# Segment attention with batch norm: bounds of the segments by products with a search matrix, and the first list ahead of the other tables

## The chip, the cores and the metric

The kernel runs on one core of a Trainium2 chip. The time is the device time of one execution in microseconds (us); the profile's span, from the first to the last instruction, is some microseconds shorter. The core has five engines that run their own instruction streams and meet at semaphores: PE (TensorE, matrix products), DVE (VectorE), ACT (ScalarE), POOL (GpSimd, which here issues gathers and scatters by index) and SP (SyncE, which here issues plain transfers).

## The reference

16,384 tokens with 256 features each carry a segment number from 0 to 7 (`bids`), in no order. The reference lets every token attend to the tokens that its segment holds in a padded table, and normalises the result over all tokens:

```python
q, k, v = feat @ Wq, feat @ Wk, feat @ Wv          # 32, 32 and 256 wide
starts = jnp.searchsorted(bids, jnp.arange(8))     # a binary search in bids as they stand
pos = jnp.arange(N) - starts[bids]
def pad(x): return jnp.zeros((8, 3072, x.shape[-1])).at[bids, pos].set(x)
scores = jnp.einsum('bld,bmd->blm', pad(q), pad(k))          # unset keys masked by -1e9
rp = jnp.einsum('blm,bmd->bld', softmax(scores), pad(v))
t = rp[bids, pos] @ Wt
tn = (t - t.mean(0)) / jnp.sqrt(t.var(0) + 1e-5) * gamma + beta
return feat + jax.nn.relu(tn)
```

Because `bids` isn't sorted, the search ends where a binary search in an unsorted row happens to end, and most positions fall outside the table of 3,072 slots or wrap to its other end. A token that owns a slot is called an owner; each segment has some 500 to 700 of them here. All other tokens read a slot at one of a table's edges.

## The kernel before

**Tables.** `bids` lies in a tile of 128 partitions by 128 tokens (`b_i`, `b_f`). For each segment a start is found by two binary searches on DVE (`search`, L758 to L764): seven rounds over the first tokens of the partitions (`lo_p`), a product that fetches the row found (`ps_row`), and seven rounds within that row (`lo_j`); the result is `st_bc`. From it follow each token's position (`pos`), the owners (`own`, L794 to L803), how often each row of the result is read (`reads`, written to DRAM at L811), and for each segment a running count of its owners (`lcx`, nine scans at L816, the ninth for tokens that lost their slot to another). Two products give each partition's first rank and the totals (`ps_c`, L822). The largest total, read into registers as `n_max` (L857), decides at L863 whether this path or a general one runs.

**Lists.** `load_list(e)` makes the list of segment e. DVE marks which partition holds each rank (`oh`, L906 to L912), PE multiplies these marks with `lcx` in FP32 (`pc`, L936), DVE compares counts with ranks (`upto`, L947) and adds up the token's number (`idx`, L952). POOL then gathers the tokens' rows (`xs`) and their counts of reads (`reads_r`) from DRAM, one indirect DMA for 128 rows (L892).

**Attention.** Segments are worked one after the other, in tiles of 128 tokens: four tiles if there are fewer than 512 owners, else six. `tc.Switch` over four bits (twice, for segments 0 to 3 and 4 to 7) picks code for these lengths. `project(b)` transposes the rows (`px`, L974, copied to `xT` by ACT and DVE), forms queries and keys (`pqk`, L985) and values (`pv`, L1004); `scores` forms `s` and ACT its exponentials (`pr_a`, `pr_b`); `sums` forms a tile's weighted sum (`po`, L1051), divides it (`rdens`), subtracts a reference row (`tk`, L1056), and adds its first and second moments, weighted by `reads_r`, to `acc` (L1059 and L1065, with ACT's square between). `reference_row` makes that row as the mean of segment 0's values.

The program writes segment 0's list, project(0), its first scores, the reference row and the list of segment 1; then for each segment b: project(b+1), load_list(b+2), attend(b), first scores of b+1, and at b = 0, 1, 2 and 4 the tables of edges and of the losers. A scheduler orders each engine's instructions from that; between the arms of a Switch nothing moves.

**End.** The moments give a scale and a shift (`sums`, L1320); then all of `feat` passes through SBUF in 16 transfers of 1 MB each way, the edges' value is added by a product with a selection matrix (`hot`), and POOL scatters the owners' rows over the result.

Of the kernel before, what the change touches and what calls it, by code (L numbers as in the profile page):

```python
# [9 lines left out]
F32 = mybir.dt.float32  # L10
# [8 lines left out]
P = 128  # L19
NB = 8  # L20
# [511 lines left out]
def segment_attention_bn_kernel(  # L532
# [43 lines left out]
    with ExitStack() as short:  # L576
# [13 lines left out]
        nc.vector.memset(eps_t, EPS)  # L590
        nil = keep.tile([P, 1], F32, name="nil")
        nc.vector.memset(nil, 0.0)
        ones = keep.tile([P, P], F32, name="ones")
        nc.vector.memset(ones, 1.0)
# [3 lines left out]
        lcx = keep.tile([P, NL, J + 2], F32, name="lcx")  # L598
        cend = keep.tile([P, NL], F32, name="cend")
        n_bc = keep.tile([P, NL], F32, name="n_bc")  # L600
        iota_r = keep.tile([P, FW], F32, name="iota_r")
        rcol = keep.tile([P, FT], F32, name="rcol")
        irow = keep.tile([P, P], F32, name="irow")
        pcol = keep.tile([P, 1], F32, name="pcol")
        emod = keep.tile([P, 1], F32, name="emod")
        later_part = keep.tile([P, 2], F32, name="later_part")
        st_bc = keep.tile([P, NB], F32, name="st_bc")
        arm_i = keep.tile([1, 1], I32, name="arm_i")
        tiles_i = keep.tile([1, NB // PART], I32, name="tiles_i")
        ident = keep.tile([P, P], F32, name="ident")  # L610
        ecol = keep.tile([P, NB], F32, name="ecol")
        b_f = keep.tile([P, J], F32, name="b_f")

# [20 lines left out]
        def tmp(name):  # L634
            return keep.tile([P, J], F32, name=name)

        pos, below, above, own = tmp("pos"), tmp("below"), tmp("above"), tmp("own")
        cbeg = keep.tile([P, NL], F32, name="cbeg")

        def over_j(x, n=NB):  # L640
            return x.unsqueeze(2).to_broadcast([P, n, J])

        def over_e(x, n=NB):
            return x.unsqueeze(1).to_broadcast([P, n, J])
# [4 lines left out]
        with ExitStack() as prep:  # L649
            pp = prep.enter_context(tc.tile_pool(name="prep", bufs=1))  # L650
            pps = prep.enter_context(tc.tile_pool(name="prep_ps", bufs=1, space=PSUM))

            b_i = pp.tile([P, J], I32, name="b_i")
            bids2 = bids.rearrange("(p j) -> p j", j=J)
            nc.sync.dma_start(b_i, bids2)
            PS = LMAX // J
            bs_i = pp.tile([P, J], I32, name="bs_i")
            nc.vector.memset(bs_i, -1)
            nc.sync.dma_start(bs_i[0 : P - PS, :], bids2[PS:P, :])
            br_i = pp.tile([P, J], I32, name="br_i")  # L660
            nc.vector.memset(br_i, -1)
            nc.sync.dma_start(br_i[PS:P, :], bids2[0 : P - PS, :])
            wv_sb = pp.tile([P, DH, D], F32, name="wv_sb")
            nc.scalar.dma_start(wv_sb, wv.rearrange("(h p) m -> p h m", p=P))
            wt_sb = pp.tile([P, DH, D], F32, name="wt_sb")
            nc.scalar.dma_start(wt_sb, wt.rearrange("(h p) m -> p h m", p=P))
            for i, w in enumerate((wq, wq, wk, wk)):
                nc.scalar.dma_start(wqk[:, :, ts(i, DQ)], w.rearrange("(h p) m -> p h m", p=P))
            nc.scalar.dma_start(gamma_bc, gamma.unsqueeze(0).to_broadcast([P, D]))
            nc.scalar.dma_start(beta_bc, beta.unsqueeze(0).to_broadcast([P, D]))  # L670


            def iota_f(dst, pattern, base, mult, shape, name):
                raw = pp.tile(shape, I32, name=name)
                nc.gpsimd.iota(raw, pattern=pattern, base=base, channel_multiplier=mult)
                nc.vector.tensor_copy(dst, raw)
                return raw

            iota_f(irow, [[1, P]], 0, 0, [P, P], "irow_i")
            pcol_i = iota_f(pcol, [[0, 1]], 0, 1, [P, 1], "pcol_i")  # L680
            make_identity(nc, ident)
            m3 = pp.tile([P, NB, J], F32, name="m3")
            w3 = pp.tile([P, NB, J], F32, name="w3")
            o3 = pp.tile([P, NL, J], F32, name="o3")
            iota_f(ecol, [[1, NB]], 0, 0, [P, NB], "ecol_i")
            tok = pp.tile([P, J], F32, name="tok")
            iota_f(tok, [[1, J]], 0, J, [P, J], "tok_i")
            iota_f(rcol, [[P, FT]], 0, 1, [P, FT], "rcol_i")
            iota_f(iota_r, [[1, FW]], 0, 0, [P, FW], "iota_r_i")
            emod_i = pp.tile([P, 1], I32, name="emod_i")  # L690
            nc.vector.tensor_scalar(emod_i, pcol_i, NE - 1, None, ALU.bitwise_and)
            nc.vector.tensor_copy(emod, emod_i)
            part_i = pp.tile([P, 1], I32, name="part_i")
            nc.vector.tensor_scalar(part_i, pcol_i, 3 * NE, None, ALU.bitwise_and)
            nc.vector.tensor_scalar(later_part[:, 0:1], part_i, NE, None, ALU.is_ge)
            nc.vector.tensor_scalar(later_part[:, 1:2], part_i, 2 * NE, None, ALU.is_ge)

            def zero(x):
                nc.scalar.copy(x, nil.to_broadcast([P, x.shape[1]]))

            for b in range(NB):
                zero(xs[:, ts(b, FT), :].rearrange("p t d -> p (t d)"))
            for b in range(NB):
                zero(tk[:, b * FT + TMIN : (b + 1) * FT, :].rearrange("p t d -> p (t d)"))
            for x in (acc, E, xL, L):
                zero(x.rearrange("p t d -> p (t d)"))
            nc.vector.memset(reads_r, 0.0)
            nc.vector.memset(rdens, 1.0)
            nc.vector.memset(ridL, NB * FW)
            powers = pp.tile([1, NB], F32, name="powers")  # L710
            for b in range(NB):
                nc.gpsimd.memset(powers[:, b : b + 1], float(1 << (b % PART)))

            tri = pp.tile([P, P], F32, name="tri")
            nc.vector.tensor_scalar(tri, irow, pcol, None, ALU.is_gt)
            later = pp.tile([P, J], F32, name="later")
            nc.vector.tensor_scalar(later, irow, 0.0, None, ALU.is_gt)


            wvT = pp.tile([P, DH, D], F32, name="wvT")  # L720
            for m in range(DH):
                ps = pps.tile([P, D], F32, tag="w", name=f"ps_wvT{m}")
                for h in range(DH):
                    nc.tensor.transpose(ps[:, ts(h, P)], wv_sb[:, h, ts(m, P)], ident)
                nc.scalar.copy(wvT[:, m, :], ps)
            for h in range(DH):
                ps = pps.tile([P, D], F32, tag="w", name=f"ps_wvt{h}")
                for m in range(DH):
                    nc.tensor.matmul(
                        ps, wvT[:, m, ts(h, P)], wt_sb[:, m, :], start=(m == 0), stop=(m == DH - 1)  # L730
                    )
                nc.scalar.copy(wvt[:, h, :], ps)

            nc.vector.tensor_copy(b_f, b_i)
            bs_f = pp.tile([P, J], F32, name="bs_f")
            nc.vector.tensor_copy(bs_f, bs_i)

            first = pp.tile([P, NB], F32, name="first")  # L740
            nc.vector.tensor_copy(first, b_f[:, 0:1].to_broadcast([P, NB]))
            ps_first = pps.tile([NB, P], F32, tag="s", name="ps_first")
            nc.tensor.matmul(ps_first, first, ident, start=True, stop=True)

            less = pp.tile([NB, P], F32, name="less")
            hit = pp.tile([NB, P], F32, name="hit")
            mid = pp.tile([NB, 1], F32, name="mid")
            go = pp.tile([NB, 1], F32, name="go")
            lo_p = pp.tile([NB, 1], F32, name="lo_p")
            lo_j = pp.tile([NB, 1], F32, name="lo_j")  # L750

            def at_mid(where):
                nc.vector.scalar_tensor_tensor(
                    hit, irow[0:NB, :], where, less, ALU.is_equal, ALU.mult, accum_out=go
                )

            def search(lo):
                nc.vector.memset(lo, 0.0)  # L758
                w = P // 2
                while w:  # L760
                    nc.vector.tensor_scalar(mid, lo, float(w), None, ALU.add)
                    at_mid(mid)
                    nc.vector.scalar_tensor_tensor(lo, go, float(w), lo, ALU.mult, ALU.add)
                    w //= 2  # L764

            nc.vector.tensor_scalar(less, ps_first, pcol[0:NB, :], None, ALU.is_lt)
            search(lo_p)
            sel = pp.tile([NB, P], F32, name="sel")
# [713 lines left out]
```

## Time and profile before

| what | value |
|---|---|
| time | 438.07 us, median of 3 (436.2 to 439.6) |
| span of the profiled run | 432.9 us |
| busy: PE, DVE, POOL, ACT | 313.1, 274.3, 167.8, 110.1 us |
| mean granted clock of PE | 0.799 |
| first gather of rows | at 40.20 us |
| first queries and keys | at 51.30 us |
| first transfer of the last stage | at 311.02 us |

Busy time is the time in which an engine had an instruction under way. A slice's digit is its busy share in tenths. In a timeline the first number is the start and the second the duration in us, `xN` the number of merged instructions (an FP32 product is recorded as two), and brackets give the idle time of the engine just before and what ended it. PEclk is the clock that PE was granted, 1.00 being full.

### The profile page before, as it was taken

The page shows a single profiled execution, that of the slowest core. Times are in us where ns is not written, and L with a number is a line of the kernel's source. Part 1 is how long each engine was busy: PE and PEld are TensorE (multiplying, and loading weights), DVE is VectorE, ACT ScalarE, POOL GpSimd, SP SyncE. Part 2 cuts the span into 40 slices and gives each one's busy share as a digit, 9 for nine tenths or more (in the row PEclk, how much of TensorE's full clock was granted, in tenths as well). Part 3 has the DMA queues.
Part 4 walks back from the last instruction along what each step waited for, and adds up shares of the span by engine and source line. Part 5 has one row for each costly group of instructions (what it writes and reads, how often), then busy time and mean ns, then how long its engine had stood idle before and what let it go on. Part 6 is the DMA issues. An engine that isn't in the chain of part 4 may idle for free. (4 is left out here: it accounts for less than half of the span.)

```text
span 432.9 us, 4300 instructions
## 1 busy us (share of the span) xinstructions
PE 313.1 (72%) x1195; PEld 197.4 (46%) x1195; DVE 274.3 (63%) x801; ACT 110.1 (25%) x205; POOL 167.8 (39%) x179
## 2 busy tenths in 40 slices
PE   1143684996697999999599989999706888989200
PEld 0022253763363687587267757776302333334000
DVE  6796124996962267556457954646479866596950
ACT  5930131230222333342343135144010111111000
POOL 2002714868037046527001844701020053776770
PEclk9996597998697799999579999999855675555555
DMA  4000101030013013003202301102495999999940
GB/s 101 1 6 14 30 1 47 12 115 17 4 29 113 0 38 104 21 24 106 61 0 85 114 26 36 59 24 86 128 420 241 341 380 402 401 388 415 381 162 2
DMA packets 21485, 53.38 MB, mean 123 GB/s; under 512 B 6606, under 2 KB 14112, under 8 KB 17322
## 3 DMA queue, kind: packets, MB, share of 16 engines
q1 hardware_dynamic: 10474, 24.98, 16.1%
q10 hardware_dynamic: 4224, 17.70, 10.3%
q0 software_dynamic: 6720, 10.02, 7.5%
q14 instruction: 51, 0.42, 0.3%
q8 instruction: 16, 0.26, 0.3%
HBM read 26.67 MB, written 29.92 MB: 131 GB/s over the span
## 5 line engine op out<-in xcount | busy, mean ns | idle before, releaser
L892 POOL DMA_INDIRECT xs<-in_r_feat,idx x48 | 53.3, 1110 | 115.4 <-DVE upto L947 98.0
L1051 PE MATMUL po<-vs,pr_a 128*128 128x257 f32 x320 | 78.3, 391 | 2.9 <-ACT pr_a L1023 2.3
L1413 POOL DMA_INDIRECT out<-tk,idx x48 | 47.3, 985 | 54.4 <-DMA out<-f 36.7
L1051 PEld LDWEIGHTS po<-vs,pr_a 128*128 128x128 f32 x320 | 59.3, 193 | 17.3 <-issue 4.4
L892 POOL DMA_INDIRECT reads_r<-reads_of,idx x48 | 51.8, 1078 | 14.6 <-issue 14.6
L1385 PE MATMUL pf<-y,hot 48*128 48x256 bf16 x128 | 35.2, 381 | 23.0 <-DVE f L1396 11.4
L1396 DVE TENSOR_TENSOR f<-f,pf 128x512 f32<-128x512 f32 x48 | 30.9, 683 | 16.7 <-PE pf L1385 16.6
L1018 PE MATMUL s<-q,k 32*128 32x512 f32 (+1 forms) x128 | 36.8, 593 | 6.0 <-DVE q L995 6.0
L1004 PE MATMUL pv<-wvt,xT 128*128 128x256 f32 x168 | 40.8, 398 | 0.0
L974 PE MATMUL px<-ident,xs 128*128 128x128 f32 x84 | 20.4, 350 | 26.5 <-DMA xs<-in_r_feat,idx 18.7
L1004 PEld LDWEIGHTS pv<-wvt,xT 128*128 128x128 f32 x168 | 32.9, 199 | 9.9 <-ACT q L996 2.8
L1385 PEld LDWEIGHTS <-hot 48*128 48x128 bf16 x128 | 13.7, 118 | 51.0 <-issue 47.6
L1390 PE MATMUL pf<-f,ident 128*128 128x256 f32 x64 | 35.4, 663 | 1.4 <-DMA f<-in_r_feat 1.4
L1064 ACT ACTIVATE sq<-tk 128x256 f32<-128x256 f32 x40 | 16.7, 417 | 69.8 <-DVE tk L1056 62.7
L974 PEld LDWEIGHTS px<-ident,xs 128*128 128x128 f32 x84 | 11.7, 170 | 42.6 <-issue 19.6
L1023 ACT ACTIVATE pr_a<-s,mask 128x512 f32<-128x512 f32 x40 | 24.7, 687 | 17.8 <-PE s L1018 17.7
L1394 ACT COPY f<-pf 128x512 f32<-128x512 f32 x16 | 9.4, 586 | 72.1 <-PE pf L1390 46.8
L978 DVE COPY xT<-px 128x256 f32<-128x256 f32 x21 | 8.9, 422 | 29.5 <-PE px L974 29.5
L985 PE MATMUL pqk<-xT,wqk 128*128 128x512 f32 (+1 forms) x52 | 25.4, 634 | 0.1
L1051 PE MATMUL po<-vs,pr_b 128*128 128x257 f32 x96 | 21.8, 381 | 0.3 <-DVE tk L1056 0.3
L992 DVE COPY k<-pqk 32x128 f32<-32x128 f32 x42 | 12.2, 291 | 14.0 <-PE pqk L985 13.1
L1390 PEld LDWEIGHTS pf<-f,ident 128*128 128x128 f32 x64 | 15.4, 292 | 12.2 <-issue 7.6
(240 smaller groups left out, 431.6 us busy)
## 6 DMA issues: line engine op xcount, KB each, us to landing
f<-in_r_feat SPq DMA_DIRECT2D x16, 1024.0 KB, 10.0
out<-f ACTq DMA_DIRECT2D x16, 1024.0 KB, 9.8
t_rows<-tk SPq DMA_DIRECT2D x4, 768.0 KB, 4.7
t_rows<-tk SPq DMA_DIRECT2D x4, 512.0 KB, 2.9
eb<-edge_of SPq DMA_DIRECT2D x16, 96.0 KB, 2.4
t_rows<-tk SPq DMA_DIRECT2D x4, 256.0 KB, 2.1
xs<-in_r_feat,idx POOLq DMA_INDIRECT x48, 2.8
reads_r<-reads_of,idx POOLq DMA_INDIRECT x48, 2.4
```

What stands on the lines that cost most here:

```text
L892: nc.gpsimd.indirect_dma_start(out=dst, out_offset=None, in_=table, in_offset=bass.IndirectOffsetOnAxis(ap=ind, axis=0), bounds_check=n - ...
L974: nc.tensor.transpose(px[:, ts(t, P)], xs[:, b * FT + t0 + t, ts(h, P)], ident)
L985: nc.tensor.matmul(pqk[:, 0:w], wqk[:, h, :], xT[:, h, own_c], start=(h == 0), stop=(h == DH - 1),)
L1004: nc.tensor.matmul(pv[:, t, :], xT[:, h, ts(t0 + t, P)], wvt[:, h, :], start=(h == 0), stop=(h == DH - 1),)
L1018: nc.tensor.matmul(s[:, i, 0:w], k[g, t // 4, :], q[g, c : c + w], start=True, stop=True)
L1023: nc.scalar.activation((pr_b if c else pr_a)[:, t, 0:w], s[:, i, 0:w], AF.Exp, bias=mask[:, m : m + 1],)
L1051: nc.tensor.matmul(po, pr[:, t, ts(r, P)], v[:, t, :], start=(t == 0), stop=(t == T - 1))
L1064: nc.scalar.activation(sq, tk[:, at, :], AF.Square)
L1385: nc.tensor.matmul(pf[:, u, :], hot[r, g % (NG // 2), i + u, :], y3[r, :], start=True, stop=not on_pe,)
L1390: nc.tensor.matmul(pf[:, u, :], ident, two[:, u, :], start=False, stop=True)
L1396: nc.vector.tensor_add(two, two, pf)
L1413: w = nc.gpsimd.indirect_dma_start(out=out, out_offset=bass.IndirectOffsetOnAxis(ap=idx[:, at : at + 1], axis=0), in_=y, in_offset=None, b ...
```

## The change

Four things are changed, all for the time until the rows of the first segments are on chip.

1. The two binary searches become products. A binary search visits a known set of places, so a matrix `path` of 128 by 128 entries tells, for the comparisons of all places at once, which end the search reaches: the place where the product equals its least possible value (`path_min`).
2. Ownership of segment e is decided without `pos`: two comparisons of the token's place with bounds from the segment's start (`begin`, `end`), for one segment at a time, so that segment 0's count, list and gathers come ahead of all other tables. The order on DVE and PE is written out by hand for this part; `positions` (with `reads`) follows project(0), the losers' count `others` follows segment 0, and the branch on `n_max` goes: the same condition now ends in `bad`, which is looked at after the end as before. `reference_row` takes one tile instead of six. Segments 0 and 1 and 2 have their lists made ahead of the Switch, and segment b's stage makes the list of b+3.
3. The counts `lcx`, the marks `oh` and the segment masks `m3`, `o3` are BF16 instead of FP32 (ranks are split into a high and a low part), and `token_tables` reuses `m3` and `o3`.
4. The moments of segment b are added in the stage of segment b+1 (`moment`), save for segments 3 and 7, which end a Switch. The gathers of `reads_r` are a part of their own (`load_reads`). Zeroing the two unused tiles of `tk` moves from the start into the stage of each short segment.

```diff
-            def search(lo):
-                nc.vector.memset(lo, 0.0)
-                w = P // 2
-                while w:
-                    nc.vector.tensor_scalar(mid, lo, float(w), None, ALU.add)
-                    at_mid(mid)
-                    nc.vector.scalar_tensor_tensor(lo, go, float(w), lo, ALU.mult, ALU.add)
-                    w //= 2
+        def visits(name, less):
+            ps = ps_o.tile([P, NB], F32, tag="po", name=f"ps_{name}")
+            nc.tensor.matmul(ps, path, less, start=True, stop=True)
+            return ps
+
+        def ends(name, ps):
+            sel = tmp(name, NB, BF16)
+            nc.vector.tensor_scalar(sel, ps, path_min, None, ALU.is_equal)
+            return sel
...
+        def owners(e):
+            one = slice(e, e + 1)
+            nc.vector.scalar_tensor_tensor(
+                o3[:, e, :], place, begin[:, one], m3[:, e, :], ALU.is_ge, ALU.mult
+            )
+            nc.vector.scalar_tensor_tensor(
+                o3[:, e, :], irow_b, end[:, one], o3[:, e, :], ALU.is_lt, ALU.mult
+            )
+            count(e, o3[:, e, :])
...
-        lcx = keep.tile([P, NL, J + 2], F32, name="lcx")
+        lcx = keep.tile([P, NL, J + 3], BF16, name="lcx")
...
-                    oh = fw.tile([P, FW], F32, tag="oh", name=f"oh_{e}", bufs=1)
+            oh = fw.tile([P, FW], BF16, tag="oh", name=f"oh_{e}")
...
+        with tc.manual_schedule(engines={mybir.EngineType.DVE, mybir.EngineType.PE}):
+            paths()
...
+            sel_p = ends("sel_p", ps_p)
+            ps_row = ps_o.tile([P, NB], F32, tag="po", name="ps_row")
+            nc.tensor.matmul(ps_row, b_b, sel_p, start=True, stop=True)
...
+            owners(0)
+            ps_0 = ranks(0, 1)
+            nc.vector.tensor_copy(st_bc, ps_st)
+            owners(1)
+            ranks_kept(0, 1, ps_0)
+            oh = list_masks(0, FT)
+            pcs = [list_places(0, h, oh) for h in range(FT // 3)]
+            for e in range(2, 4):
+                owners(e)
+            for h, pc in enumerate(pcs):
+                list_tokens(0, h, pc)
+            weights()
+            for e in range(4, NB):
+                owners(e)
+            ps_1 = ranks(1, NB)
...
+            ranks_kept(1, NB, ps_1)
+            load_list(1)
+        tc.no_sync_barrier()
...
         project(0, FT)
         first_scores(0)
         reference_row()
+        positions()
+        load_reads(0)
+        load_list(2)
+        load_reads(1)
...
+                    if b + 3 < NB:
+                        load_list(b + 3)
                     if b + 2 < NB:
-                        load_list(b + 2, FT, xs[:, ts(b + 2, FT), :])
+                        load_reads(b + 2)
+                    if i:
+                        for u in range(T[i - 1]):
+                            moment((b - 1) * FT + u)
                     attend(b, T[i])
```

## The prediction

> **What bounds the kernel now.** I read the slices first, then the windows by stage, then the timelines of PE, POOL and DVE. The slices cut 432.9 us into 40 parts of 10.8 us:
>
> ```profile
> PE   1143684996697999999599989999706888989200
> POOL 2002714868037046527001844701020053776770
> DMA  4000101030013013003202301102495999999940
> ```
>
> Three regimes show. Slices 1 to 4: PE nearly idle, DVE at work. Slices 5 to 28: PE busy with a few holes. From 310 us: the DMA row at 9. The windows (length, then busy time of PE, PEld, DVE, ACT and POOL, granted clock, DMA share, GB/s) price them:
>
> ```profile
> 8.50:22.00 13.50, 1.45 (x5) 0.77 (x5) 10.36 (x66) 13.50 (x16) 0.00 (x0) 1.00 0.02 3
> 76.00:100.00 24.00, 22.51 (x97) 15.21 (x96) 23.81 (x66) 6.80 (x15) 17.30 (x15) 0.96 0.20 62
> 160.00:190.00 30.00, 29.99 (x141) 21.70 (x141) 15.59 (x51) 10.38 (x21) 15.07 (x16) 1.00 0.17 50
> 310.00:433.00 123.00, 70.58 (x196) 29.84 (x196) 83.54 (x144) 11.17 (x18) 53.23 (x54) 0.53 0.81 316
> ```
>
> The start is a serial chain on DVE; segment 0 fills DVE (23.8 of 24 us); later segments fill PE (30.0 of 30); the end, 123 us, is bound by DMA, begins after the last segment, and the change leaves it alone. So a microsecond counts if it moves the last segment's end. What PE waits for on its way there (start, duration, operation, idle before it):
>
> ```profile
> 51.30 4.15 PE L985 MATMUL pqk<-xT,wqk 128*128 128x512 f32 x8
> 67.34 1.50 PE L936 MATMUL pc<-lcx,oh 128*128 128x130 f32 x12
> 73.25 0.45 PE L974 MATMUL px<-ident,xs 128*128 128x128 f32 x1 [4.42 <-DMA xs<-in_r_feat,idx]
> 75.05 0.90 PE L974 MATMUL px<-ident,xs 128*128 128x128 f32 x3 [1.35 <-DMA xs<-in_r_feat,idx]
> 102.32 0.47 PE L974 MATMUL px<-ident,xs 128*128 128x128 f32 x1 [2.47 <-DMA xs<-in_r_feat,idx]
> 112.53 2.07 PE L1018 MATMUL s<-q,k 32*128 32x512 f32 x2 [4.84 <-DVE q L995]
> 135.97 0.90 PE L974 MATMUL px<-ident,xs 128*128 128x128 f32 x3 [2.69 <-DMA xs<-in_r_feat,idx]
> ```
>
> Real work begins at 51.30 (queries of segment 0); four later waits are for gathered rows, one is for DVE. POOL and DVE tell why:
>
> ```profile
> 40.20 1.20 POOL L892 DMA_INDIRECT xs<-in_r_feat,idx  x1 [5.29 <-DVE idx L952]
> 70.11 1.00 POOL L892 DMA_INDIRECT xs<-in_r_feat,idx  x1 [14.40 <-DVE upto L947]
> 75.15 0.62 DVE L906 TENSOR_SCALAR oh<-iota_r,lcx 128x768 f32<-128x768 f32 x1 [4.39 <-issue]
> ```
>
> The first row gather waits until 40.20 for `idx`; segment 1's until 70.11, since its list products stand behind all of project(0) on PE. The 4.39 us is the Switch on DVE; the new kernel keeps it.
>
> [...]the trace has FP32 only (twelve records of `pc` in 1.77 us at full clock, at 153.66). [...]the trace's 128x1024 products take 1,210 to 1,227. [...]the pair of `s` took 2.07 us after the 4.84 us hole and 1.13 elsewhere[...].[...]
>
> **Part 1, the start (to the first gather).** Before: two binary searches, 14 rounds of 0.74 us on DVE (8.6 to 20.7), then `pos` (1.23 + 1.93), ownership, nine scans and the n_max branch, all ahead of list 0. After, in the built order: ten path operations (1.3 to 3.1; small ones 0.18 apart, 128x128 ones 0.2 to 0.3), then four DVE-PE-DVE trips (`ps_min`, `sel_p`, `ps_row`, `sel_j`) and the pair `ps_st`. FP32 trips of this size take 0.37 (`selT`) to 0.69 us (`ps_row`); I take 0.4 to 0.5 in BF16. With 0.15 to 0.3 us operations between: `begin`/`end` at 7.5. owners(0): 0.3 + 0.3 + 0.42 = 1.0, to 8.6; owners(1) covers the `ranks` trip, to 9.7; five small copies, to 10.3; list masks 0.69 + 1.03, to 12.0; valid and mask, owners(2) and (3), 2.3, to 14.3; the first half list (as 38.43 to 39.91 before, one subtraction more) 1.9, to 16.2. **First gather 16.4 for 40.2: 23.8 us earlier.** The eight zero copies of `xs` (1.38 us apart on ACT) start near 2.5, so segment 0's slot is clear in time.
>
> **Part 2, to the queries of segment 0.** Six gathers 1.3 us apart end at 23.9 and land at 25.1, no longer interleaved with `reads`. But DVE's fixed order puts ahead of `xT`: the second half list (to 18.0), owners(4) to (7), 4.1 (22.1), ranks 1.2 (23.3), the masks of list 1, 1.7 (25.0), its tokens, 4.0 (29.0), then small bits and the 1.23 us product of `positions` (30.7). The three DVE `xT` copies are split by its 1.93 us reduction and by 0.9 of masks: they end at 31.1, 33.4 and 34.6. The weight products (two chains of 2.1 us, from about 17 when ACT ends its zeros) hide before `ps_1`. **Queries at 34.7 for 51.3: 16.6 us earlier**; 7 of the 23.8 are given back.
>
> **Part 3, to segment 1's transposes.** From the queries to the end of `pr0` took 16.2 us (67.5). Now `pr0` has one tile instead of six: 3.4 falls to about 0.6, so 13.4, to 48.1. Then list 2's BF16 products (0.7 for 1.5), its tokens on DVE and the Switch, the same 7.7 us as before (67.5 to 75.15): DVE enters segment 0 at 55.8, **19.3 us earlier**. List 1's rows (gathers 27.3 to 35) are there, so the 1.35 us wait goes too; DVE sets the pace.
>
> **Part 4, segments 0 and 1, bound by DVE.** From 75.15 to the queries of segment 2 at 113.5, DVE was busy about 34.8 us and idle 3.6. The built order of the arm these lengths take (4, 4, 6, 6 tiles: the two `pr_b` groups at 164 and 198) moves segment 0's eight moment operations behind those queries (3.3), drops the two 1024-wide `m3t`, `o3t` (2.3), adds others() and a second `lr` (1.7): about 31 us, and the `k` copies no longer alternate with table products. s(2) starts at about 86 for 112.5: **26.5 earlier**. POOL must follow: `reads` is written near 42 to 44, twelve `reads_r` gathers take 15.6 (to 60), list 2's six to 68; its transposes come near 74. Enough by 6 us.
>
> **Part 5, segments 2 to 7, bound by PE.** List 3 is now gathered a segment earlier, so the 2.69 us hole and the half clock behind it (pqk 5.37 for 2.7, s 2.07 for 1.13: 3.6) go: 6.3. Segment 1's list products save 1.1; its moments and edge tables now follow in one run beside PE (about +1). Lists 5, 6, 7 and the short one save 1.1 each where PE is full: 3.9. Moments a segment later cost DVE the same work; the last segment still has its own, so the tail is equal. Zeroing `tk` (0.53 us each) moves to ACT, which is a quarter busy, but two copies stand ahead of `xT` at the second Switch: +0.6. Sum: 26.5 + 1.1 - 1 + 6.3 + 3.9 - 0.6 = **36.2 us**.
>
> 438.1 - 36.2 = 401.9: **402 us**.
>
> **Rivals.** (a) *The head start stops at the DVE-bound part*: `reads` lands late, POOL serves twelve reads ahead of list 2, PE meets a new hole with half clock in segment 1, or table work again cuts up `k`. Then the 19.3 us of part 3 are kept and little else: 438.1 - 19.3 = 419. For it: DVE at 23.8 of 24 us; against: 6 us of slack. (b) *More*: BF16 quickens masks, owners and segment tests (half of some 6 us ahead of the queries), and PE, without holes, saves the half clock in segment 2 (pv 7.55 for 5.45, s 2.07 for 1.13: 3 us) and twice 2 us at the second Switch: 402 - 10 = 392. (c) *Slower*: PE, packed more densely, is granted less. At 0.83, as between 100 and 160 us, some 200 us of PE-bound work grow by 200 x (1/0.83 - 1) = 41: 402 + 41 = 443. Against it: full clock from 160 to 190 with no pause.
>
> **How the numbers follow.** Forecast 402: 0.65. (a) 419: 0.20. (b) 392: 0.12. (c) 443: 0.03. Unknowns: BF16 trips, 0.3 to 0.69 over five trips, is 2 us;[...] POOL's gathers, 1.0 each or stretched to the 2.85 seen at 98.30, a few us. With (a) and (b) inside: 390 to 419. Faster by over 1%: 0.95; within: 0.02; slower: 0.03.
>
> **What would show it.** Right: first gather near 16, first 512-wide `pqk` near 35, segment 0's DVE work from 56, no wait for `xs` after segment 0, transfers at 9 tenths from about 275 for the same 123 us. Wrong: PE waiting for `xs` of segment 2, a DVE wait on `reads_r` ahead of the moments, PEclk under 9 in segments 3 to 6, or a last stage longer than 123 us.

## The result, and the profile after

The changed kernel takes **389.85 us** (median of four runs, 386.95 to 398.45), the kernel before 437.13 beside it: a ratio of 0.889, 95% interval 0.881 to 0.897. Here and below, ratios and the times of the experiments leave out runs over 1.5% above the fastest of the same kernel; one of these four was such a run. The forecast was 402, between 390 and 419: the change gave more than forecast. The span fell from 432.9 to 386.6 us, by 46.3, where the forecast summed 36.2. The slices of the changed kernel (a slice is 9.7 us now):

```profile
PE   1347849889999999769997999974058877897100
POOL 3257477888747735600285000013000527776770
PEclk9986959999999999957999999995555785555555
DMA  5011002121502301310251010217949999999820
```

PE is at work from the fourth slice on, the DMA row reaches 9 some 40 us earlier, and the clock row shows what the forecast priced too low: from slice 7 to 17 it stays at 9. The 5 and 7 behind it are the second Switch, as before. The windows put numbers to it. First the kernel before (DVE's entry into segment 0 to the second Switch; segment 3's transposes and queries within it), then the changed kernel for the same work, and its end stage; the columns are those of the windows above.

```profile
75.15:203.50 128.35, 115.87 (x481) 81.85 (x481) 82.70 (x281) 36.02 (x76) 65.51 (x60) 0.91 0.16 48
...
130.01:146.37 16.36, 13.67 (x33) 6.64 (x33) 4.45 (x21) 2.47 (x6) 8.18 (x9) 0.69 0.23 74
```

```profile
54.00:160.00 106.00, 99.25 (x453) 71.07 (x453) 81.48 (x307) 35.42 (x75) 73.08 (x66) 0.97 0.21 62
...
97.39:105.60 8.21, 8.21 (x31) 4.30 (x31) 7.15 (x28) 2.23 (x6) 6.41 (x6) 1.00 0.51 151
...
263.30:386.60 123.30, 67.91 (x198) 29.24 (x198) 83.71 (x145) 11.17 (x18) 53.36 (x54) 0.56 0.80 315
```

Where PE slowed down, the granted clock was 0.50: in the kernel before from 112.53 to 117 and from 135.97 to 142, in the changed one from 50 to 58 and from 168.02 to 173. There a pair of scores took 2.07 us for 1.12. That is called half clock here; in the experiments it is mostly read from durations such as these. A mean of 0.91 over 128 us is then some 23 us at half clock (2 x 0.09 x 128.35); 0.97 over 106 us is some 6. For nearly the same products PE was busy 115.87 us and is busy 99.25: 4.9 of these 16.6 us are the list products, and 8 of the rest (half of 23 less 6, an estimate) are that clock. The timelines of PE, POOL and DVE, at the places shown before:

```profile
32.60 4.29 PE L915 MATMUL pqk<-xT,wqk 128*128 128x512 f32 x8
...
83.93 1.12 PE L948 MATMUL s<-q,k 32*128 32x512 f32 x2 [1.75 <-DVE q L925]
84.98 5.45 PE L934 MATMUL pv<-wvt,xT 128*128 128x256 f32 x24
...
97.39 0.66 PE L904 MATMUL px<-ident,xs 128*128 128x128 f32 x4 [0.42 <-DVE wE L1097]
...
102.75 2.85 PE L915 MATMUL pqk<-xT,wqk 128*128 128x512 f32 x8
```

```profile
16.66 1.25 POOL L821 DMA_INDIRECT xs<-in_r_feat,idx  x1 [12.55 <-ACT L L716]
```

```profile
54.00 0.79 DVE L834 TENSOR_SCALAR oh<-iota_r,cbeg 128x768 bf16<-128x768 f32 x1 [4.52 <-issue]
```

No wait for `xs` follows segment 0. The hole (idle time of PE) ahead of segment 2's scores is 1.75 us for 4.84, and the products behind it run at full clock (1.00 from 83.93 to 90.43). The account, by the starts of the same work in both traces:

| stretch | forecast gain | measured |
|---|---|---|
| to DVE's entry into segment 0 (75.15, 54.00) | 19.3 | 21.2 |
| on to the scores of segment 2 (112.53, 83.93) | 7.2 | 7.4 |
| on to segment 3's transposes (130.01, 97.39) | 0.1 | 4.0 |
| on to the end of segment 3's 512-wide queries (146.37, 105.60) | 6.3 | 8.2 |
| on to the second Switch (203.50, 159.96) | with the one but next: 3.9 | 2.8 |
| the second Switch, to the end of segment 5's 512-wide queries (222.50, 178.94) | -0.6 | 0.0 |
| on to the last `e_late`, a product of the last segment (306.61, 258.99) | see above | 4.1 |
| the rest (span 432.9, 386.6) | 0 | -1.3 |

So less than half of the gain lies ahead of segment 0's attention, where the change was aimed.

In the comparisons of the experiments below the kernel before took 455 to 470 us and the changed one 415 to 422, and the profiles of the changed and the edited kernels have idle stretches of 3 to 14 us whose release isn't recorded, above all behind the first Switch. What causes them was not found. The gain there is 37 to 40 us, where the first comparison had 49 (437.1 less 388.5). Each experiment is therefore read against the changed kernel of its own comparison where there is one, and by stretches without such idling.

### The profile page after: what moved, and what is told of

The parts are those of the page before. It is cut to its first block, busy times and chain, and to the rows that moved or that the text cites. A ratio compares the mean times of both kernels' runs of the same rounds, so it can differ in the third digit from the quotient of the medians.

```text
span 386.6 us, 4158 instructions
## 1 busy us (share of the span) xinstructions
PE 284.2 (74%) x1135; PEld 179.7 (46%) x1135; DVE 266.8 (69%) x792; ACT 107.9 (28%) x201; POOL 173.4 (45%) x180
## 5 line engine op out<-in xcount | busy, mean ns | idle before, releaser
L821 POOL DMA_INDIRECT xs<-in_r_feat,idx x48 | 58.6, 1220 | 66.3 <-DVE upto L871 36.6
L821 POOL DMA_INDIRECT reads_r<-reads_of,idx x48 | 50.9, 1060 | 21.5 <-issue 12.8
L1429 PE MATMUL pf<-y,hot 48*128 48x256 bf16 x128 | 33.8, 365 | 25.1 <-DVE f L1440 13.4
L934 PE MATMUL pv<-wvt,xT 128*128 128x256 f32 x168 | 38.7, 383 | 0.0
L934 PEld LDWEIGHTS pv<-wvt,xT 128*128 128x128 f32 x168 | 31.3, 190 | 8.6 <-ACT q L926 2.1
L1434 PE MATMUL pf<-f,ident 128*128 128x256 f32 x64 | 33.3, 628 | 2.2 <-DMA f<-in_r_feat 2.2
L948 PE MATMUL s<-q,k 32*128 32x512 f32 (+1 forms) x128 | 32.4, 570 | 2.9 <-DVE q L925 2.9
L978 ACT ACTIVATE sq<-tk 128x256 f32<-128x256 f32 x40 | 16.6, 417 | 62.8 <-DVE tk L994 56.2
L904 PE MATMUL px<-ident,xs 128*128 128x128 f32 x84 | 18.1, 333 | 17.3 <-DVE xT L908 8.0
L904 PEld LDWEIGHTS px<-ident,xs 128*128 128x128 f32 x84 | 10.9, 164 | 29.9 <-issue 12.8
L993 DVE RECIPROCAL rdens<-po 128x1 f32<-128x1 f32 x40 | 6.5, 164 | 23.6 <-PE po L989 23.5
L821 POOL DMA_INDIRECT E<-t_rows,eidx x1 | 1.1, 1108 | 43.5 <-issue 43.5
L1434 PEld LDWEIGHTS pf<-f,ident 128*128 128x128 f32 x64 | 14.6, 277 | 12.7 <-issue 6.9
```

Of the source, the lines that this page charges most:

```text
L821: nc.gpsimd.indirect_dma_start(out=dst, out_offset=None, in_=table, in_offset=bass.IndirectOffsetOnAxis(ap=ind, axis=0), bounds_check=n - ...
L904: nc.tensor.transpose(px[:, ts(t, P)], xs[:, b * FT + t0 + t, ts(h, P)], ident)
L934: nc.tensor.matmul(pv[:, t, :], xT[:, h, ts(t0 + t, P)], wvt[:, h, :], start=(h == 0), stop=(h == DH - 1),)
L948: nc.tensor.matmul(s[:, i, 0:w], k[g, t // 4, :], q[g, c : c + w], start=True, stop=True)
L978: nc.scalar.activation(sq, tk[:, at, :], AF.Square)
L1429: nc.tensor.matmul(pf[:, u, :], hot[r, g % (NG // 2), i + u, :], y3[r, :], start=True, stop=not on_pe,)
```

## The experiments

**The changed kernel again**, to see whom the idle stretches belong to.

> The changed kernel once more, as the measure for the runs beside it on the same chip. The four runs ahead of this one ran on a chip where the kernel before took 469.6 us, against 437 to 438 elsewhere, with idle stretches of 3 to 13 us behind the first Switch for which the profile names no cause of the program. My theory (those stretches belong to that chip's executions, the kernel before has them too): the ratio to the kernel before is 0.889 as in the first comparison, or a few per cent closer to one where the stretches are there. Rival (they belong to the edited kernels): the changed kernel is free of them on any chip.

Measured: 419.5 us, 456.6 before, ratio 0.920 (0.911 to 0.928). The changed kernel has the stretches too, so the edits don't make them; the kernel before has no profile there. Three more comparisons gave 0.914, 0.913 and 0.913.

**The old searches in the new order.**

```diff
-            paths()
...
-            ps_p = visits("sel_p", less)
+            search(lo_p)
...
+            search(lo_j)
```

> The changed kernel with the two old binary searches (14 rounds of three DVE operations) in the place of the products with the search matrix; everything else, the order of the lists too, stays. In the trace of the changed kernel `begin` starts at 6.78 us; with the searches (14 x 0.74, two small transposes, the segment tests behind them) it should start near 18.0, 11.2 us later. My theory (a start that is one DVE chain passes one to one to the last segment's end): first gather near 27.9, first 512-wide queries near 43.8, segment 0's DVE work from about 65, whole time 390 + 11.2 = 401. Rival (slack behind the start swallows part of it, since POOL and the gathers run ahead): first gather as late, but the whole time only 394 to 397.

> The kernel with the old binary searches again, beside the changed kernel on one chip. My theory (the start passes one for one): first gather 12.3 us later, as in the first run of it, and the last segment's end and the whole time later by the same 11 to 14 us. Rival (part of a head start is absorbed by slack behind it): the end later by under 9 us.

The first run had no changed kernel beside it (434.5 us, ratio to before 0.926); first gather at 29.00, queries at 44.65. The second: 426.2 us against 415.1, so 11.0 more (ratios to before 0.938, 0.931 to 0.945, and 0.913, 0.905 to 0.922). Against the changed kernel beside it the first gather is 12.3 us later, the queries of segment 0 11.6, those of segments 2 to 5 9.2, 11.9, 9.7 and 9.8, and `ps_bad`, the product behind the last segment, 9.6. About 10 of the 12 us pass to the end. The whole time fits my theory, the last segment's end lies between it and the rival.

**The lists as late as before.**

```diff
-        load_list(2)
...
-                    if b + 3 < NB:
-                        load_list(b + 3)
                     if b + 2 < NB:
+                        load_list(b + 2)
                         load_reads(b + 2)
```

> The changed kernel with the lists as late as before: list b+2 is made in stage b, and list 2 no longer ahead of the first Switch. My theory (the advance of the lists is what closed the holes): the wait for gathered rows of segment 3 is back, 2 to 4 us, with half-clock work behind it (queries 5.3 for 2.8, scores 2.07 for 1.12: 3.6 us), and one more list product lies in the part that PE fills (0.6); against this the first Switch starts some 2.7 us earlier, since list 2 is no longer ahead of it. Whole time about 390 + 3 + 3.6 + 0.6 - 2.7 = 394.5. Rival (the earlier start alone gave POOL the room, and the advance does nothing): no hole, the earlier Switch is kept, 387 to 388.

Measured: 429.7 us, with no changed kernel on that chip; the total decides nothing. Its PE timeline does:

```profile
106.47 0.70 PE L904 MATMUL px<-ident,xs 128*128 128x128 f32 x3 [2.89 <-DMA xs<-in_r_feat,idx]
...
108.82 2.07 PE L948 MATMUL s<-q,k 32*128 32x512 f32 x2
...
116.06 4.98 PE L915 MATMUL pqk<-xT,wqk 128*128 128x512 f32 x8
```

The wait for segment 3's rows is back with 2.89 us, and what follows runs at half clock (scores 2.07 us for 1.12, queries 4.98 for 2.85; the granted clock is 0.62 on average from 103 to 121.2). From the first transpose (103.28) to the end of these queries takes 17.7 us; the same stretch takes 8.3 (120.50 to 128.77) in the next kernel on this chip, the one with the moments in their own segment, 8.2 in the changed kernel and 16.4 before. So the earlier list is worth 8 to 9.4 us there, of which the wait itself is about a third and the half clock more than half. Segment 2 waits as well, 4.21 us for its rows at 80.40: POOL gathered the second half of list 2 only at 77.57, with three gathers of `reads_r` between the halves. From DVE's entry (51.13) to segment 2's scores (89.76) this run takes 38.6 us, without one of the unrecorded idle stretches in it; the kernel before took 37.4, the changed one in the first comparison 29.9. So the earlier list is a condition of the gain there too.

**The moments in their own segment.**

```diff
-            if b % PART == PART - 1:
-                moment(at)
+            moment(at)
...
-                    if i:
-                        for u in range(T[i - 1]):
-                            moment((b - 1) * FT + u)
```

> The changed kernel with the moments of each tile in its own segment again. My theory (segment 0 is DVE-bound, segment 1's rest and all later ones PE-bound): the eight moment operations of segment 0 (0.48 us each, 3.8) come back ahead of the queries of segment 2, whose scores move from 83.9 to about 87.5, and nothing is won back where PE is full: 390 + 3.5 = 393.5. Rival 1 (DVE has room in segment 0): 390 to 391. Rival 2 (the moments then wait for `reads_r`, which POOL fetches between 43 and 59 us, and hold up everything behind them on DVE): 396 or more, with a DVE wait on reads_r in segment 0.

> The kernel with the moments in their own segment again, beside the changed kernel on one chip. My theory: eight operations of 0.48 us come back into the DVE-bound segment 0, +3.5 us at the scores of segment 2 and at the end. Rival 1: DVE has room, 0 to 1. Rival 2 (the moments wait for reads_r or crowd DVE in segment 1 as well, so that transposes or lists come late[...]): +6 and more, with a hole and half-clock work in segment 2.

First run 427.4 us, nothing beside it; second 427.5 us against 422.2, ratios to before 0.933 (0.926 to 0.940) and 0.914 (0.902 to 0.926), which just touch; the traces say more. My theory is right for the scores of segment 2 (3.45 us later) and too small for what follows them; Rival 2 is nearer, though no wait for `reads_r` shows: DVE's order does it. Its timeline in segment 1, with the moments back:

```profile
98.96 0.28 DVE L922 COPY k<-pqk 32x128 f32<-32x128 f32 x1
99.17 1.20 DVE L1072 TENSOR_REDUCE both<-w 128x8 f32<-128x1024 f32 x1
100.40 0.29 DVE L922 COPY k<-pqk 32x128 f32<-32x128 f32 x1
100.72 1.23 DVE L1071 TENSOR_TENSOR w<-m,above 128x1024 f32<-128x1024 bf16 x1
```

and PE behind it, first in this kernel, then in the changed kernel beside it:

```profile
104.62 1.64 PE L948 MATMUL s<-q,k 32*128 32x512 f32 x2 [4.83 <-DVE q L925]
106.19 8.26 PE L934 MATMUL pv<-wvt,xT 128*128 128x256 f32 x24
```

```profile
101.17 1.12 PE L948 MATMUL s<-q,k 32*128 32x512 f32 x2 [1.67 <-DVE q L925]
102.22 5.45 PE L934 MATMUL pv<-wvt,xT 128*128 128x256 f32 x24
```

3.8 us of moments ahead push three long table operations back until they fall between the four `k` copies, as in the kernel before. The queries start at the same time in both (96.61 and 96.75), so PE waits longer: 4.83 us, the same as before the change (4.84). Then it does the values at half clock. From the queries to segment 3's transposes: 24.95 us (96.61 to 121.56) for 18.50 (96.75 to 115.25), at a mean granted clock of 0.86 for 1.00. Of these 6.4 us some 3.2 are the longer hole, as the sum of DVE's work has it, and 3.3 the half clock behind it (scores 1.64 for 1.12, values 8.26 for 5.45); the forecast had only the 3.3 us of DVE.

The second half is not safe. In the kernel with FP32 lists, which keeps the moments late, the same hole was followed by half clock:

```profile
104.19 1.12 PE L948 MATMUL s<-q,k 32*128 32x512 f32 x2 [1.66 <-DVE q L925]
105.24 7.13 PE L934 MATMUL pv<-wvt,xT 128*128 128x256 f32 x24
```

**Counts and list products in FP32**, with the matrix that adds up the counts.

```diff
-        lcx = keep.tile([P, NL, J + 3], BF16, name="lcx")
+        lcx = keep.tile([P, NL, J + 3], F32, name="lcx")
...
-        tri = tmp("tri", P, BF16)
+        tri = tmp("tri", P)
...
-            oh = fw.tile([P, FW], BF16, tag="oh", name=f"oh_{e}")
+            oh = fw.tile([P, FW], F32, tag="oh", name=f"oh_{e}")
```

> The kernel with counts, masks and list products in FP32 again, now beside the changed kernel on one chip. My theory: six list products 1.77 for 0.57 us; +7.5 us on the changed kernel, of which the start has 2 and the stages from segment 1 on 5.4. Rival 1 (BF16 quickens DVE too): over 10. Rival 2 (the products hide behind DVE): under 3.

Measured: 433.5 us against 422.2 (ratios 0.937, 0.931 to 0.943, and 0.914, 0.902 to 0.926), as the first run of it (433.7). `ps_bad` comes 5.4 us later in the profiled runs, less than my 7.5; the rest of the 11.3 us lies in the end stage, which the edit doesn't touch. The whole time alone would point to Rival 1, but the 128x768 marks take DVE 0.61 and 1.01 us in both, so BF16 didn't quicken them. One list product, in FP32 and then in BF16 (count, then the shortest, median and longest in ns):

```profile
L851 PE MATMUL pc<-lcx,oh x102: 272/275/586, 11.7 to 221.9; 128*128 128x131 f32 x102
```

```profile
L851 PE MATMUL pc<-lcx,oh x51: 220/222/319, 11.6 to 216.7; 128*128 128x131 bf16 x51
```

An FP32 product is two records of 275 ns, a BF16 one a single record of 222. These records overlap: twelve in a row took 1.77 us before, six take 0.52 at full clock.

**Filling PE's idle time behind the second Switch.**

```diff
+                if b == PART + 1 and t0 == 0:
+                    warm = ps_o.tile([P, D + 1], F32, tag="po", name="warm")
+                    for _ in range(12):
+                        nc.tensor.matmul(warm[:, 0:P], ident, ident, start=True, stop=True)
```

> The changed kernel with twelve products of the identity with itself (no use is made of them) on PE between the first and the second pair of transposes behind the second Switch, where PE stands for 3.02 us because DVE's xT copy is late. The wait is as long as before, PE only isn't idle in it. My theory (the idle time itself puts PE at half clock): the next transposes start as late as before, but the pairs of scores behind them take 1.12 us instead of 2.07, the queries of segment 5 2.75 instead of 5.33, and the last segment ends 3 to 4 us earlier than in the changed kernel. Rival (the slow work behind a hole has another cause, a limit on the granted clock or late operands): same 2.07 and 5.33, and no gain.

> The changed kernel with 22 filling products behind the first transposes of segment 5 instead of 12, so that PE works until DVE's late xT copy is there; they may delay the next transposes by up to 0.5 us. My theory[...]: with PE busy from its Switch on, the scores take 1.12 us and the queries 2.75 to 2.9 instead of 2.07 and 5.3, and the stretch from the first transposes behind the Switch to the end of the queries is 11 to 12 us instead of 14.8 to 15.6. Rival (the Switch's own 2.1 us, or something else than idle time, does it): still 2.07 and over 4, no gain.

With twelve (420.4 us against 422.2) the products ended at 193.0 and the next transposes came at 194.70: a hole of 1.70 us was left, and scores and queries took 2.07 and 5.49. A miss. With 22:

```profile
185.99 1.09 PE L904 MATMUL px<-ident,xs 128*128 128x128 f32 x4 [2.50 <-ACT pr_a L957]
186.87 6.21 PE L912 MATMUL warm<-ident 128*128 128x128 f32 x44
192.92 0.60 PE L904 MATMUL px<-ident,xs 128*128 128x128 f32 x4
193.45 1.12 PE L952 MATMUL s<-q,k 32*128 32x512 f32 x2
```

Beside it the changed kernel has

```profile
188.29 1.08 PE L904 MATMUL px<-ident,xs 128*128 128x128 f32 x4 [2.21 <-ACT pr_a L953]
189.31 2.07 PE L948 MATMUL s<-q,k 32*128 32x512 f32 x2
193.13 1.26 PE L904 MATMUL px<-ident,xs 128*128 128x128 f32 x4 [1.75 <-DVE xT L908]
194.33 2.07 PE L948 MATMUL s<-q,k 32*128 32x512 f32 x2
```

In both, the Switch's own wait (2.50 and 2.21 us) already put PE at half clock: its transposes take 1.09 and 1.08 us for 0.66. So the rival is right about where the half clock begins here. With the filling PE is back at full clock some 3 us after that wait (an estimate: its 44 records took 6.21 us, 1 us more than at the 0.118 each of the 24 in the kernel with twelve), and the scores take 1.12; with a second wait, of 1.75 us, the scores behind it take 2.07 and the queries 4.35. So in these two profiles half clock came with the idle time, and it ended in the one where PE had work without a pause. There is no gain (417.9 us against 415.1): the filling took 6.2 us, held the transposes up by 2.1, and the stretch from the first transposes to the end of the queries is 15.1 us for 14.6. The waits must go; filling them doesn't pay.

**ACT relieved behind the second Switch.** The square root's table load goes, and the zeroing of `tk` is moved behind the first sums.

```diff
-            if T == TMIN:
-                zero(tk[:, b * FT + TMIN : (b + 1) * FT, :].rearrange("p t d -> p (t d)"))
...
+                if u == T - 1 and T == TMIN:
+                    zero(tk[:, b * FT + TMIN : (b + 1) * FT, :].rearrange("p t d -> p (t d)"))
...
-                nc.scalar.activation(root, eps_t, AF.Sqrt)
+                nc.scalar.activation(root, E[:, 1, 0:1], AF.Sqrt)
```

> The changed kernel with ACT relieved behind the second Switch: the square root that loads its table early takes its operand from the last segment's moments, so that it can't go ahead of segment 5 (two table loads of 1.28 us leave the way of the xT copies), and the tk rows that no query has are zeroed behind the first sums instead of ahead of the copies (0.62 us each). Theory 1 (ACT makes the 3.02 us hole): hole about 1 us, half of the half-clock work behind it gone, 3 to 4 us: 386 to 387. Theory 2 (DVE makes it: its Switch ends at 165.95 and 1.6 us of list masks stand ahead of its xT copy): the hole stays above 2 us, 389 to 390.

Measured: three of its four runs took 419.6 to 422.1 us, one 410.3, beside 419.5, so the whole time decides nothing. The profile (of a run of 422.1 us) has a hole of 1.36 us for 1.35 ahead of the second transposes, and 14.6 us for 14.5 from the first transposes to the end of the queries. The load of the square root's table (1.28 us in the changed kernel's trace, at 169.22) is gone from there, but the two zeroing copies still stand ahead of the `xT` copies (192.19, 192.98). And the hole of 3.02 us that both theories speak of was 1.35 here without the edit. No gain shows, and in both profiles the second transposes wait for DVE's copy, which speaks for Theory 2; it isn't settled.

**A reordered start**, from what is left of the start: `xT` copies of segment 0 stand behind list 1's tokens, and list 2's behind the reference row.

```diff
-            load_list(1)
-        tc.no_sync_barrier()
+            oh = list_masks(1, FT)
+            pcs = [list_places(1, h, oh, ps_o, "po") for h in range(FT // 3)]
+            turn(0, FT, act_only=True)
...
+            for h, pc in enumerate(pcs):
+                list_tokens(1, h, pc)
```

> The changed kernel with project(0) in the part ordered by hand, ahead of the tokens of list 1; the products of lists 1 and 2 in the other PSUM pool, so that they hold no buffer of the transposes; all xT copies of segment 0 on ACT; list 2's tokens ahead of the reference row. My theory (the start is still one DVE chain, in which these stand in each other's way): transposes at 25.5 instead of 27.0, first 512-wide queries at 29.5 instead of 32.6, DVE enters segment 0 at about 49 instead of 54.0, and the end follows by about 5 us: 385 where the changed kernel takes 390 (ratio to it 0.987). Rival (segment 0 is then held up by POOL: the twelve reads gathers, now behind list 2's, or by list 1's rows): entry at 49 but the scores of segment 2 no earlier than 82, 388 to 390.

> The two last edits together, and the last list made one segment earlier still, ahead of the second Switch, so that its masks (1.6 us) do not stand ahead of segment 5's xT copies on DVE; the two 0.91 us fills of eb go to POOL. Theory: 5 us from the start, and at the second Switch the hole of 3.02 us and the half-clock work behind it (scores 2.07 for 1.12, queries 5.33 for 2.75) fall to the Switch's own 2.2 us: together about 10 us, 380 where the changed kernel takes 390 (ratio to it 0.974). Rival (the Switch's own wait keeps PE at half clock in any case): 384 to 385.

> The reordered start, mended: PE goes from the queries of segment 0 straight to its values, which need no copy of DVE, then the reference row (after the first pair of values), and the scores last; the masks of list 2 stand behind the copies of queries and keys. In the first reordered start the queries came 3.5 us earlier, but PE waited 1.78 us and did scores and values at half clock (2.75 and 7.55 us for 1.13 and 5.45), and nothing was left. My theory: PE stays at full clock, values 5.45, DVE enters segment 0 at about 50.5 instead of 54, and the end follows by 3 to 4 us (ratio to the changed kernel about 0.991). Rival (POOL, with list 2 ahead of the reads, or DVE's Switch takes it back): no difference at the end.

> The mended start in five rounds. My theory (the start is still the bound, and its 2.5 to 3.5 us pass to the end): 3 to 4 us under the changed kernel beside it. Rival (the 3.4 us of the three rounds were scatter): within 1.5 us of it.

The first took 408.2 to 423.8 us in its four runs, beside 419.5 for the changed kernel: too scattered to tell. In its profile (of a run of 423.8 us) queries came at 29.12, but PE then waited 1.78 us for DVE's copies, and

```profile
39.26 7.55 PE L941 MATMUL pv<-wvt,xT 128*128 128x256 f32 x24
```

shows the values at half clock: the reference row was no earlier (47.5 for 46.7). The next kernel, with the Switch edits added, has the same start, 1.78 us and then 7.05. It took 425.2 us; DVE stands 5.8 and 8.2 us without a recorded cause in its segment 3, so it tells nothing of these edits. In the mended order PE still waits 2.57 us until the copies of queries and keys free a buffer, but then runs the values at full clock, in 1.99 and 3.62 us; DVE enters segment 0 at 51.94 (54.99 beside it):

```profile
38.41 3.62 PE L944 MATMUL pv<-wvt,xT 128*128 128x256 f32 x16
```

411.0 us against 415.1 in three rounds, 418.0 against 422.2 in five. Both are some 4 us less, as expected, but the intervals of the ratios to before overlap (in five rounds 0.904, 0.895 to 0.913, and 0.913, 0.900 to 0.925): likely, not settled.

## What the forecast had right, and the step that failed

**Parts 1 to 3** held to about 2 us: first gather 16.66 (forecast 16.4), queries of segment 0 at 32.60 (34.7), DVE's entry at 54.00 (55.8). Of the 2.1 us at the queries, list 1's tokens took 3.3 instead of 4.0 (25.12 to 28.46), and the last `xT` copy followed at 33.27. A BF16 mask beside an FP32 table saved DVE nothing: the 1024-wide product took 1.20 us (1.23 before). The BF16 list products took a third of the time of the FP32 ones (0.52 us for 1.77); the 0.7 for 1.5 of the forecast and its 1.1 us for each list were the author's estimates, since the traces before had FP32 products only.

**Part 4** held in sum (7.4 for 7.2), and POOL followed as forecast: `reads_r` to 58.6, list 2 to 67.4, transposes at 73.74. The moments experiment confirms its price for the moments (3.3 us, 3.45 measured at the scores), and the late lists show that it needs the earlier list 2 as well. What it left out is what PE then saves: the forecast noted that `k` copies no longer alternate with table work, and gave the shorter hole no price on PE.

**Part 5 is the step that failed**, in its size: it summed 9.7 us from the scores of segment 2 to the last segment's end, and the account has 19.1 there (its third to seventh rows). It priced half clock behind holes too low, in two places:

```profile
114.53 7.55 PE L1004 MATMUL pv<-wvt,xT 128*128 128x256 f32 x24
...
141.00 5.37 PE L985 MATMUL pqk<-xT,wqk 128*128 128x512 f32 x8
```

The values of segment 2 stood behind the 4.84 us hole, which Part 4 made shorter. Their half clock and that of the scores (7.55 for 5.45, 2.07 for 1.12: 3.05 us) was left to the rival "more", although the forecast had read the slower scores behind this very hole from the trace. Together with the +1 us for edge tables, which PE never saw, this makes the 3.9 us that are missing in the third row of the account. In the fourth row, 6.3 forecast and 8.2 measured, the forecast counted the queries and one pair of scores behind segment 3's hole; two groups of transposes (0.90 and 1.12 us) and a second pair of scores (1.22) had run at half clock as well, another 1.3 us.

The list products behind segment 3's queries were forecast at 3.9 us, 1.1 for each of 3.5 lists. They gave 2.8 for 2.5 lists up to the second Switch, and 2.9 in the last stretch, where one of two lists has gone altogether because it is made a segment earlier. The other 1.2 us of that stretch weren't traced.

In the kernel before, half clock followed shorter holes than that of 4.84 us as well: those of 2.47 and 2.69 us (granted clock 0.50 from 102.30 to 104 and from 135.97 to 142). The forecast itself priced the half clock behind the second. So its sum has what follows segment 3's hole, and not what follows segment 2's.

**The rivals.** (a) didn't come: no wait for rows, no new hole; the moments experiment shows how near it was. (b), 392, came closest in size, but that is luck for the most part: of its 10 us only the 3 of segment 2's half clock came, and the FP32 run shows that these can be absent. DVE's marks gained nothing by BF16, and the second Switch is as long as before (19.0 us); list products and segment 3 made up the difference. (c) didn't come: the clock is granted in full from 74 to 160 us (1.00 in that window). The end stage is unchanged (123.3 us).

## What to carry to other kernels

Price a wait on PE together with the work at half clock that can follow it, and do it for every wait that an edit removes or shortens, not only for the one it was made for: here the half clock was more than half of the 8 to 9.4 us that the earlier list brought, the wait itself 2.7 to 2.9. Work put ahead on DVE, here 3.8 us of moments, can push long operations (1.20 to 1.23 us here) between the small copies that PE needs; the sum of busy times gave the delay rightly, but only the built order shows the hole that it makes on PE (4.83 us for 1.67). Bringing PE's input forward without its next operands gave a new wait of 1.78 us and half clock (7.55 us for the values, 5.45 in the changed kernel), and the reference row was no earlier.

## What was not expected of the hardware

The length of a hole alone didn't decide whether half clock followed. With PE at full clock before, holes of 1.66 us (FP32 lists), 2.21 (the changed kernel beside 22 filling products), 2.47 and 2.69 (the kernel before) led to it. Holes of 1.67 and 1.75 ahead of the same scores (the changed kernel beside the FP32 lists and in the first comparison), of 2.21 (the changed kernel in the first comparison) and of 2.57 and 3.06 (the mended start) did not. With twelve filling products, two holes of 2.13 and 1.70 us with 2.84 us of work between them led to it behind the second. The longest holes, 47 of 3.70 to 14.26 us between 40 and 280 us in the 18 profiles that were followed that far, all had half clock behind them. What decides for the shorter ones wasn't found.

And the same two programs took 4 to 9% longer in later comparisons, with idle stretches of which the profile names no cause.
